# Interleaving side stages with a selective scan: another place on TensorE, earlier loads, another pacing rule

## The chip, the cores and the metric

The kernel runs on one core of a Trainium2 chip. The metric is the device time in microseconds (us) from the first to the last work of one execution. The kernel before took 11,412.55 us, the median of three runs (11,408.17 to 11,425.88). A core has five instruction streams that matter here: TensorE (PE in the profile; its weight loads are PEld), VectorE (DVE), ScalarE (ACT), GpSimd (POOL) and SyncE (SP), which issues every DMA of this kernel. Each works through its own queue in order.

## The reference, cut to what matters

Four images of 64 x 64 positions and 96 channels pass through four layers. Layer 0 and layer 1 are selective-scan blocks; layers 2 and 3 are attention without softmax, and a small feed-forward network with 8-bit rounding. Layer 1 takes a 2D Fourier transform first and its inverse after. In both blocks the core of the work is this recurrence, run in four directions over all positions, with 16 states for each channel:

```python
def step(hst, inputs):
    ul, dl, bl, cl = inputs
    dA = jnp.exp(dl[..., None] * A)
    hst = hst * dA + (dl * ul)[..., None] * bl[:, :, None, :]
    y = jnp.einsum('bkdn,bkn->bkd', hst, cl)
    return (hst, y)
```

Around it stand an input projection, a 3 x 3 convolution per channel, SiLU, small projections that give delta, B and C, and afterwards a layer norm, a gate (SiLU of a second projection) and an output projection.

## The kernel before, in words

**The scans.** The recurrence is cut into phases: two for layer 0 (two images packed in the 128 partitions each) and four for layer 1 (one image each). A phase has four directions; each direction is cut into segments of positions, eight of 512 in layer 0, and five of 512, 512, 384, 384 and 320 in layer 1. A segment has 12 steps: four groups of four states (q) times three chunks of 128 channels (c). So there are 384 steps in each of the first two phases and 240 in each of the other four, 1728 in all. A step runs four scans on VectorE (line 676), one per state.

For each scan ScalarE makes the decay, an exponential (`exp`, line 648; `front_x` for states 0 and 1, `front_y` for states 2 and 3, the latter in PSUM). The input term of states 0 and 1 is made position-major on ScalarE (`make_bx`, line 612) and turned by TensorE (`transposed`, line 644): these are the b transposes. For states 2 and 3 GpSimd multiplies it (`front_b`, line 666). The outputs are multiplied by C on GpSimd (`multiply`, line 713) or VectorE (`multiply_kept`, line 694), and TensorE adds them up in PSUM by transposing matmuls (`accumulate`, line 723). B and C come as broadcasts by DMA (line 590), two buffers each.

PSUM has eight banks: three for the accumulators, three (`ab0` to `ab2`) that the b transposes and the decays of states 2 and 3 share in turn, one for preparing the next segment (`pp`), and one (`ms`) for everything else. So transposes for state 0 of the next step wait until scan 1 of this step is done with its bank, and those for state 1 until scan 2 is.

**The side stages.** While a phase is scanned, stages of other images are woven in: for example the normalisation and projection of the second pair (`begin0`), its gate (`gate0`), the flip to the other direction (`flip`), the norm and output projection of a finished phase (`end0`, `end1`), the Fourier transform (`fourier`), its inverse, and the two transformer layers (`tokens`). Each is a Python generator; what lies between two `yield`s is a piece. `Env` keeps the stages in a queue, and `Env.step` issues one piece. A piece can ask for a place: `yield LATE` means only the last slot of a step, `yield BURST` means the place for a long ScalarE instruction (`burst`, after which a step's second slot is held back). A copy out of PSUM is deferred: it is issued at the next piece (`E.flush`).

Each of the four engines' orders is written out by hand (the loop over `steps`, line 809). A step has three slots, where `slot` issues one piece of the next segment's preparation (`prepare`) and, when the counter `due` has reached 1, one side piece. `due` grows in each slot by a third of the phase's rate, up to 3. The rates (`RATES`) are 1.75, 2.5, and 3.0 for the rest. On TensorE a step's order was: accumulations, transposes for state 0 of the next step, first slot, transposes for state 1, second slot, last slot. A stage that a phase needs is forced to its end before (`E.require`); what remains after the last scan is issued by `E.finish`.

Before and after the scans the first projection and the last stages run alone, several workers at once (`wide=4`): the head and the tail.

**Loads of side stages.** A stage loads its inputs through SP. `visits` loads rows of x two blocks ahead, but starts anew for each part and chunk: two loads, three empty pieces, then the matmuls. `flip` loads a part, waits two pieces, and has GpSimd turn it in eight LATE pieces; its input and output share two buffers (tag `h0`). `fourier` and `inverse` load two pieces ahead of the first use. `in_weights` loads a chunk's weights where the chunk begins.

Of the kernel before, what the change touches and what calls it, by code (L numbers as in the profile page):

```python
# [23 lines left out]
SM = 512  # L24
LATE, BURST = "late", "burst"

RATES = [1.75, 2.5, 3.0, 3.0, 3.0, 3.0]
EXP_LN = "natural_log_exp_and_others"


# [92 lines left out]
                active.remove(task)  # L123


class Block:


# [54 lines left out]
                    stop=(ki == cfg.KI - 1),  # L183
                )

    def visits(self, E, sp, wi, xf, blocks, half, nm, w, done):


        def load(r, n):
            x = sp.tile([CH, 2, 512], F32, name=f"xi{half}_{nm}_{r}", tag=f"xin{w}", bufs=3)  # L190
            self.nc.sync.dma_start(out=x[:, :, : n * 64], in_=xf[:, :, r * 64 : (r + n) * 64])
            return x
# [12 lines left out]

    def in_weights(self, sp, g, c, w):
        cfg = self.cfg
        wi = sp.tile([CH, cfg.KI, 2, cfg.PI], F32, name=f"{cfg.pre}_wi_{g}_{c}", tag=f"wi{w}", bufs=2)
        self.nc.sync.dma_start(out=wi, in_=self.w["inw"][:, :, :, c, :])
        return wi  # L210

    def project(self, E, g, io):

        nc, cfg = self.nc, self.cfg
        NR, xf, W = cfg.NR, io["xf"], min(E.wide, C)
        io["u"] = u = [self.dram_tile(f"u{j}", (P, C, cfg.L), g) for j in range(2)]
        PR = max(b - a for a, b in cfg.parts)

        def chunk(sp, c, w):
# [4 lines left out]
            wi = self.in_weights(sp, g, c, w)  # L226
            for p0, p1 in cfg.parts:
                nm, pr = f"{cfg.pre}_{g}_{c}_{p0}", p1 - p0
                pad = sp.tile([P, PR + 2, 66], F32, name=f"pad_{nm}", tag=f"pad{w}")
                nc.gpsimd.memset(pad[:, : pr + 2, 0:1], 0.0)  # L230
                nc.gpsimd.memset(pad[:, : pr + 2, 65:66], 0.0)
                if p0 == 0:
                    nc.gpsimd.memset(pad[:, 0, :], 0.0)
                if p1 == NR:
                    nc.gpsimd.memset(pad[:, pr + 1, :], 0.0)

                def to_pad(r, n, pi):
                    nc.scalar.copy(
                        pad[:, r - p0 + 1 : r - p0 + 1 + n, 1:65],
                        pi[:, : n * 64].rearrange("p (r w) -> p r w", w=64),  # L240
                    )

                lo, hi = max(p0 - 1, 0), min(p1 + 1, NR)
                blocks = [(r, min(8, hi - r)) for r in range(lo, hi, 8)]
                if blocks[-1][1] < 4 and len(blocks) > 1:
                    cut = hi - lo
                    k = len(blocks)
                    sizes = [cut // k + (i < cut % k) for i in range(k)]
                    blocks = [(lo + sum(sizes[:i]), s) for i, s in enumerate(sizes)]
                yield from self.visits(E, sp, wi, xf, blocks, 0, nm, w, to_pad)  # L250
                uh = sp.tile([P, PR * 64], F32, name=f"uh_{nm}", tag=f"h{w}", bufs=2)

                def to_u(r, n, pc):
                    nc.scalar.activation(
                        uh[:, (r - p0) * 64 : (r - p0 + n) * 64], pc[:, : n * 64], AF.Identity,
                        bias=self.conv_b[:, c : c + 1],
                    )

                for t in range(9 if vector else 0):
                    dy, dx = divmod(t, 3)  # L260
                    o = uh[:, : pr * 64].rearrange("p (r w) -> p r w", w=64)
                    v = pad[:, dy : dy + pr, dx : dx + 64]
# [24 lines left out]
                yield BURST  # L287
                nc.scalar.activation(uh[:, : pr * 64], uh[:, : pr * 64], AF.Silu)
                if W == 1:
                    nc.scalar.preload_act_table_set(EXP_LN)  # L290
                nc.sync.dma_start(out=u[cfg.nat][:, c, p0 * 64 : p1 * 64], in_=uh[:, : pr * 64])
                yield
                if W == 1:
                    yield from self.flip_part(sp, g, c, p0, p1, uh, u[1 - cfg.nat])

        with E.pool(f"{cfg.pre}pj{g}") as sp:
            yield from together([chunk(sp, c, c % W) for c in range(C)], W)
            if W > 1:
                nc.scalar.preload_act_table_set(EXP_LN)

    def flip_part(self, sp, g, c, p0, p1, uh, out):

# [13 lines left out]
    def flip(self, E, g, io):  # L316

        cfg = self.cfg
        PR = max(b - a for a, b in cfg.parts)
        with E.pool(f"{cfg.pre}fl{g}") as sp:  # L320
            for c in range(C):
                for p0, p1 in cfg.parts:
                    uh = sp.tile([P, PR * 64], F32, name=f"fl_{cfg.pre}_{g}_{c}_{p0}", tag="h0", bufs=2)
                    n = (p1 - p0) * 64
                    self.nc.sync.dma_start(out=uh[:, :n], in_=io["u"][cfg.nat][:, c, p0 * 64 : p1 * 64])
                    yield
                    yield
                    yield from self.flip_part(sp, g, c, p0, p1, uh, io["u"][1 - cfg.nat])
        yield

    def gate(self, E, g, io):
# [2 lines left out]
        io["gz"] = gz = self.dram_tile("gz", (P, C, cfg.L), g)  # L334
        PR = max(b - a for a, b in cfg.parts)
        with E.pool(f"{cfg.pre}gt{g}") as sp:
            for c in range(C):
                wi = self.in_weights(sp, g, c, 0)
                for p0, p1 in cfg.parts:
                    nm, pr = f"{cfg.pre}_{g}_{c}_{p0}", p1 - p0  # L340
                    zh = sp.tile([P, PR * 64], F32, name=f"zh_{nm}", tag="h0", bufs=2)
# [4 lines left out]
                    blocks = [(r, n) for r, n in cfg.rows if p0 <= r < p1]  # L346
                    yield from self.visits(E, sp, wi, io["xf"], blocks, 1, nm, 0, to_z)
# [142 lines left out]
def scans(tc, ctx, phases, ident):  # L490
# [274 lines left out]
    with tc.manual_schedule(engines=IN_ORDER):  # L765
# [20 lines left out]
        def slot(kind, hold=False):  # L786
# [22 lines left out]
        for i, st in enumerate(steps):  # L809
# [188 lines left out]
def fourier(E, cst, x, b, dram, out):  # L998
# [7 lines left out]
    with E.pool(f"ff{b}") as sp:  # L1006
# [9 lines left out]
            return t  # L1016

        nxt = load(0)
        yield
        yield  # L1020
# [33 lines left out]
def inverse(E, cst, att, x, b, x1):  # L1054
# [6 lines left out]
    with E.pool(f"fi{b}") as sp:  # L1061
# [45 lines left out]
            yield from together([channels(w * G, a, w) for w, a in enumerate(loads)], W)  # L1107
        else:
            nxt = load(0)
            yield  # L1110
            yield
# [459 lines left out]
```

## Time and profile before

| what | value |
|---|---|
| runs | 11,408.17, 11,412.55 and 11,425.88 us |
| profiled execution, its own time | 11,418.96 us |
| its span, from the first to the last instruction | 11,417.2 us |
| mean granted TensorE clock | 0.894 |
| first scan starts, last scan ends | 213.9 us, 11,011.7 us |
| phases 1 to 6 (scan to scan) | 2476.0, 2482.2, 1517.7, 1445.7, 1441.2, 1435 us |
| scans, mean of one | 1124 to 1263 ns for 512 positions |
| `multiply` on GpSimd, mean of one | 2642 ns |
| `front_b` on GpSimd, mean of one | 1169 ns |
| flip piece on GpSimd (L308), median | 627 ns |

In the profile, a group is named by line, engine and what it writes and reads (`h_l<-ab_l`). A wait stands as "who <- who released it: us in total, times, longest". In the timeline a row is start, duration, engine, line, operation, names, shapes, and in brackets the idle time before it and what ended that. The chain of waits goes back from the last instruction to whatever released it, or to the instruction before it on its engine; its share says what the end of the kernel stood on.

### The profile page before, as it was taken

Reading aid. Unit: us, or ns where it says so; the run is one execution under the profiler, and the core shown is the slowest. Engines: PE = TensorE matmul, PEld = TensorE weight load, DVE = VectorE, ACT = ScalarE, POOL = GpSimd, SP = SyncE. Lnnn points to the kernel's source line nnn. Section 1 sums busy time; section 2 is a strip of 40 time slices with the busy share of each in tenths; the row PEclk is TensorE's granted clock in tenths of the full one; section 3 lists DMA queues with packets and bytes.
Section 4 is the critical chain, followed back from the end, with each engine's and each line's share of the span. In section 5 each row is a group of like instructions: output and inputs, shape, how many; then the busy total and the mean of one; then the engine's idle time right before and its main releaser. Section 6 shows DMA issues by size and latency. Waiting matters only on the chain. (4 is left out here: it accounts for less than half of the span.)

```text
span 11417.2 us, 163659 instructions
## 1 busy us (share of the span) xinstructions
PE 9108.9 (80%) x54944; PEld 6661.7 (58%) x54944; DVE 9922.7 (87%) x10695; ACT 9367.1 (82%) x19648; POOL 9402.0 (82%) x7464
## 2 busy tenths in 40 slices
PE   5668878788888878888888888887778877887775
PEld 2555555555666656556665565665556556665554
DVE  6889999889998998999878687988999899889964
ACT  4779999999988998998768777878888798878853
POOL 2899999988988998998779688887888788888850
PEclk9889999988998999998889899998899988998887
DMA  4555554556665455555543443542244422542242
GB/s 142 131 140 127 130 132 123 144 154 167 160 166 127 130 143 130 134 140 165 156 125 122 123 133 121 172 129 88 97 121 148 110 94 97 151 130 97 87 124 40
DMA packets 1208403, 1468.94 MB, mean 129 GB/s; under 512 B 482760, under 2 KB 1020560, under 8 KB 1149064
## 3 DMA queue, kind: packets, MB, share of 16 engines
q1 hardware_dynamic: 1207559, 1458.48, 47.0%
q8 instruction: 434, 7.11, 0.3%
q14 instruction: 410, 3.35, 0.1%
HBM read 1221.74 MB, written 236.50 MB: 128 GB/s over the span
## 5 line engine op out<-in xcount | busy, mean ns | idle before, releaser
L713 POOL TENSOR_TENSOR h_l<-h_l,bc_l 128x1536 f32<-128x1536 f32 (+2 forms) x1728 | 4565.0, 2642 | 203.2 <-DVE h_l L676 87.4
L666 POOL TENSOR_TENSOR h_l<-du_l,bc_l 128x512 f32<-128x512 f32 (+2 forms) x3456 | 3964.8, 1169 | 859.1 <-PE acc_l L723 806.4
L612 ACT ACTIVATE bx_l<-dut_l,bt_l 128x192 f32<-128x192 f32 (+2 forms) x6272 | 2750.8, 499 | 0.2
L723 PE MATMUL acc_l<-ident,h_l 128*128 128x128 f32 (+1 forms) x15840 | 2365.1, 302 | 257.0 <-POOL h_l L713 255.8
L723 PEld LDWEIGHTS acc_l<-ident,h_l 128*128 128x128 f32 (+1 forms) x15840 | 2065.1, 157 | 843.2 <-POOL h_l L713 389.5
L648 ACT ACTIVATE ax_l<-delta_l,l_alog 128x512 f32<-128x512 f32 (+2 forms) x3456 | 2140.4, 667 | 0.0
L676 DVE TENSOR_TENSOR_SCAN h_l<-b_l,state_l,h_l 128x512 f32<-128x512 f32 (+2 forms) x1266 | 1398.7, 1124 | 195.5 <-ACT b_l L648 181.7
L644 PE MATMUL b_l<-ident,bx_l 128*128 128x128 f32 (+1 forms) x6830 | 1233.9, 298 | 350.8 <-DVE h_l L676 339.4
L644 PEld LDWEIGHTS b_l<-ident,bx_l 128*128 128x128 f32 (+1 forms) x6830 | 834.8, 150 | 840.3 <-DVE h_l L676 628.3
L648 ACT ACTIVATE b_l<-delta_l,l_alog 128x512 f32<-128x512 f32 (+2 forms) x1952 | 1222.8, 626 | 102.5 <-DVE k_l L694 32.0
L644 PE MATMUL ab_l<-ident,bx_l 128*128 128x128 f32 x5320 | 916.0, 301 | 278.8 <-DVE h_l L676 265.9
L723 PE MATMUL acc_l<-ident,k_l 128*128 128x128 f32 x5121 | 838.5, 294 | 340.4 <-DVE k_l L694 323.8
L676 DVE TENSOR_TENSOR_SCAN b_l<-ax_l,state_l,b_l 128x512 f32<-128x512 f32 (+2 forms) x844 | 956.0, 1133 | 136.7 <-PE b_l L644 136.2
L648 ACT ACTIVATE ab_l<-delta_l,l_alog 128x512 f32<-128x512 f32 x1328 | 914.8, 689 | 146.3 <-DVE hk_l L694 62.5
L676 DVE TENSOR_TENSOR_SCAN h_l<-ab_l,state_l,h_l 128x512 f32<-128x512 f32 x744 | 925.3, 1263 | 113.3 <-ACT ab_l L648 64.5
L644 PEld LDWEIGHTS ab_l<-ident,bx_l 128*128 128x128 f32 x5320 | 655.4, 153 | 579.4 <-DVE h_l L676 474.2
L676 DVE TENSOR_TENSOR_SCAN h_l<-ax_l,state_l,b_l 128x512 f32<-128x512 f32 (+2 forms) x844 | 953.7, 1130 | 38.6 <-PE b_l L644 37.4
L694 DVE TENSOR_TENSOR k_l<-b_l,bc_l 128x512 f32<-128x512 f32 (+2 forms) x1462 | 896.5, 613 | 62.6 <-DMA bc_l<-l_xd_l 9.1
L723 PEld LDWEIGHTS acc_l<-ident,k_l 128*128 128x128 f32 x5121 | 632.2, 150 | 437.5 <-DVE k_l L694 356.2
L723 PE MATMUL acc_l<-ident,hk_l 128*128 128x128 f32 x3984 | 647.4, 300 | 249.6 <-DVE hk_l L694 237.7
L276 PE MATMUL pc_l<-pad_l,l_dg 128*128 128x512 f32 (+2 forms) x1656 | 771.1, 560 | 40.2 <-ACT state_l L701 22.0
L694 DVE TENSOR_TENSOR hk_l<-ab_l,bc_l 128x512 f32<-128x512 f32 x996 | 688.9, 692 | 54.5 <-issue 11.1
(252 smaller groups left out, 14802.7 us busy)
## 6 DMA issues: line engine op xcount, KB each, us to landing
bc_l<-l_xd_l SPq DMA_DIRECT2D x640, 512.0 KB
bc_l<-l_xd_l SPq DMA_DIRECT2D x512, 256.0 KB
bc_l<-l_xd_l SPq DMA_DIRECT2D x128, 1024.0 KB
bc_l<-l_xd_l SPq DMA_DIRECT2D x128, 768.0 KB
us_l<-l_u SPq DMA_DIRECT2D x96, 768.0 KB
l_y<-y_l SPq DMA_DIRECT2D x288, 256.0 KB
yt_l<-l_y SPq DMA_DIRECT2D x264, 192.0 KB
yt_l<-l_y SPq DMA_DIRECT2D x128, 384.0 KB
```

Of the source, the lines that this page charges most:

```text
L276: nc.tensor.matmul(pc[:, : n * 64].rearrange("p (r w) -> p r w", w=64), diag[:, t, :], pad[:, r - p0 + dy : r - p0 + dy + n, dx : dx + 64] ...
L612: nc.scalar.activation(t[:n, b, :, ch], z.dut[:n, b, :, ch], AF.Copy, scale=z.bt[:n, b, m : m + 1])
L644: nc.tensor.transpose(pb[:, t : t + n], st.z.bx[st.q, j][:n, b, st.c], ident[:n, :n])
L648: nc.scalar.activation(out, z.delta[:, st.c, : z.S], AF.Exp, scale=z.blk.A[:, st.c, z.k, n : n + 1])
L666: nc.gpsimd.tensor_tensor(st.h[:, 1 + j, :S], st.z.du[:, st.c, :S], st.z.b[st.q][:, j, :S], ALU.mult)
L676: nc.vector.tensor_tensor_scan(h[:, ::step], a[:, ::step], b[:, ::step], 0.0 if z.first else z.state[st.c][:, n : n + 1], ALU.mult, ALU.add,)
L694: nc.vector.tensor_tensor(hk[:, : z.S], kept_at(st, j), z.c[st.q][:, j, : z.S], ALU.mult)
L713: nc.gpsimd.tensor_tensor(h, h, z.c[st.q][:, 1 : 1 + m, : z.S], ALU.mult)
L723: nc.tensor.matmul(z.acc[st.c][:m, b, :], hc[:, t : t + m], ident, start=(first and b == 0), stop=(last and b == 0), is_transpose=True,)
```

## The change

Three things change, and no arithmetic does.

1. In a step, the first slot now comes before the transposes for state 0, and the second before those for state 1.
2. Side stages load further ahead. The new class `Inputs` holds the loads of a whole projection or gate: two blocks of rows are always ahead, across parts and chunks, and eight empty pieces stand once at the start in place of three at each part. `flip` loads the next part while it turns this one, with a buffer tag of its own and eight empty pieces at the start. `fourier` and `inverse` have six empty pieces in place of two.
3. The rates are 0.15 lower, and a slot may issue a second side piece when `due` is at least 2.

```diff
-RATES = [1.75, 2.5, 3.0, 3.0, 3.0, 3.0]
+RATES = [1.6, 2.35, 2.85, 2.85, 2.85, 2.85]
...
+class Inputs:
+    def __init__(self, blk, sp, xf, chunks, half, nm, w):
+        self.blk, self.sp, self.xf, self.half, self.nm, self.w = blk, sp, xf, half, nm, w
+        self.todo = [
+            (c, r, n) for c in chunks for p0, p1 in blk.cfg.parts for r, n in blk.rows_of(p0, p1, half == 0)
+        ]
+        self.ahead, self.wi = [], {}
+        for _ in range(2):
+            self.load()
+
+    def load(self):
+        if not self.todo:
+            return
+        sp, cfg, nc = self.sp, self.blk.cfg, self.blk.nc
+        c, r, n = self.todo.pop(0)
+        if c not in self.wi:
+            t = sp.tile([CH, cfg.KI, 2, cfg.PI], F32, name=f"{cfg.pre}_wi_{self.nm}_{c}", tag=f"wi{self.w}", bufs=2)
+            nc.sync.dma_start(out=t, in_=self.blk.w["inw"][:, :, :, c, :])
+            self.wi[c] = t
...
+        nc.sync.dma_start(out=x[:, :, : n * 64], in_=self.xf[:, :, r * 64 : (r + n) * 64])
+        self.ahead.append((self.wi[c], x))
+
+    def take(self):
+        self.load()
+        return self.ahead.pop(0)
...
-        ahead = [load(*blk) for blk in blocks[:2]]
-        yield
-        yield
-        yield
-        for b, (r, n) in enumerate(blocks):
-            ahead += [load(*blk) for blk in blocks[b + 2 : b + 3]]
-            x = ahead.pop(0)
...
+        for r, n in blocks:
+            wi, x = inputs.take()
             pi = E.psum(f"pi{half}_{nm}_{r}")
             yield from self.in_proj(pi, wi, half, x, n * 64)
             E.defer(lambda r=r, n=n, pi=pi: done(r, n, pi))
...
-            yield from together([chunk(sp, c, c % W) for c in range(C)], W)
-            if W > 1:
-                nc.scalar.preload_act_table_set(EXP_LN)
+            if W == 1:
+                inputs = Inputs(self, sp, xf, range(C), 0, g, 0)
+                for _ in range(8):
+                    yield
+                for c in range(C):
+                    yield from chunk(sp, inputs, c, 0)
+                return
+            yield from together([chunk(sp, Inputs(self, sp, xf, [c], 0, g, c), c, c) for c in range(C)], W)
+            nc.scalar.preload_act_table_set(EXP_LN)
...
+        todo = [(c, p0, p1) for c in range(C) for p0, p1 in cfg.parts]
         with E.pool(f"{cfg.pre}fl{g}") as sp:
...
+            nxt = load(*todo[0])
+            for _ in range(8):
+                yield
+            for n, (c, p0, p1) in enumerate(todo):
+                uh, nxt = nxt, load(*todo[n + 1]) if n + 1 < len(todo) else None
+                yield from self.flip_part(sp, g, c, p0, p1, uh, io["u"][1 - cfg.nat])
...
             due = min(due + st.z.ph.rate / 3, 3.0)
-            if due >= 1.0:
+            for _ in range(min(int(due), 1 + (due >= 2.0))):
                 due -= E.step(kind)
...
+            slot(None)
+            if nxt:
                 transposed(nxt, 0)
-            slot(None)
             more.take(skip=long)
             scan(st, 2)
+            slot(None, hold=long)
             if nxt:
                 transposed(nxt, 1)
-            slot(None, hold=long)
             if older and older.q == NQ - 1:
                 close_chunk(older)
             scan(st, 3)
...
-            yield
-            yield
+            for _ in range(6):
+                yield
             for c0 in range(0, CH, G):
```

The gate stage takes its rows from an `Inputs` too, the cutting of rows into blocks moves into `rows_of`, and the last part of the diff stands in `fourier` and, alike, in `inverse`.

More of the change, by code (lines that the diff above doesn't have):

```diff
@@ L123, in together @@
                 active.remove(task)
+class Inputs:
[16 more added lines that the diff above has]
+            self.wi[c] = t
+        x = sp.tile(
+            [CH, 2, 512], F32, name=f"xi{self.half}_{self.nm}_{c}_{len(self.todo)}", tag=f"xin{self.w}", bufs=3
+        )
+        nc.sync.dma_start(out=x[:, :, : n * 64], in_=self.xf[:, :, r * 64 : (r + n) * 64])
[3 more added lines that the diff above has]
+        return self.ahead.pop(0)
 class Block:
@@ L184, in in_proj, with rows_of, visits @@
                 )
[L186 to L192, printed above, removed]
-        ahead = [load(*blk) for blk in blocks[:2]]
-        yield
-        yield
-        yield
-        for b, (r, n) in enumerate(blocks):
-            ahead += [load(*blk) for blk in blocks[b + 2 : b + 3]]
-            x = ahead.pop(0)
+    def rows_of(self, p0, p1, halo):
+        cfg = self.cfg
+        if not halo:
+            return [(r, n) for r, n in cfg.rows if p0 <= r < p1]
+        lo, hi = max(p0 - 1, 0), min(p1 + 1, cfg.NR)
+        blocks = [(r, min(8, hi - r)) for r in range(lo, hi, 8)]
+        if blocks[-1][1] < 4 and len(blocks) > 1:
+            cut = hi - lo
+            k = len(blocks)
+            sizes = [cut // k + (i < cut % k) for i in range(k)]
+            blocks = [(lo + sum(sizes[:i]), s) for i, s in enumerate(sizes)]
+        return blocks
+    def visits(self, E, inputs, blocks, half, nm, done):
+        for r, n in blocks:
+            wi, x = inputs.take()
             pi = E.psum(f"pi{half}_{nm}_{r}")
@@ L204, in visits @@
             yield
[L206 to L210, printed above, removed]
     def project(self, E, g, io):
@@ L219, in project, with chunk @@
         PR = max(b - a for a, b in cfg.parts)
-        def chunk(sp, c, w):
+        def chunk(sp, inputs, c, w):
             vector = W > 1 and c > 0
@@ L225, in chunk @@
                 nc.sync.dma_start(out=diag, in_=self.diag[:, c])
-            wi = self.in_weights(sp, g, c, w)
             for p0, p1 in cfg.parts:
@@ L241, in to_pad @@
                     )
[L243 to L250, printed above, removed]
+                yield from self.visits(E, inputs, self.rows_of(p0, p1, True), 0, nm, to_pad)
                 uh = sp.tile([P, PR * 64], F32, name=f"uh_{nm}", tag=f"h{w}", bufs=2)
@@ L319, in flip, with load @@
         PR = max(b - a for a, b in cfg.parts)
+        todo = [(c, p0, p1) for c in range(C) for p0, p1 in cfg.parts]
         with E.pool(f"{cfg.pre}fl{g}") as sp:
[L321 to L325, printed above, removed]
-                    yield
-                    yield
-                    yield from self.flip_part(sp, g, c, p0, p1, uh, io["u"][1 - cfg.nat])
+            def load(c, p0, p1):
+                uh = sp.tile([P, PR * 64], F32, name=f"fl_{cfg.pre}_{g}_{c}_{p0}", tag="fl", bufs=2)
+                n = (p1 - p0) * 64
+                self.nc.sync.dma_start(out=uh[:, :n], in_=io["u"][cfg.nat][:, c, p0 * 64 : p1 * 64])
+                return uh
+            nxt = load(*todo[0])
[4 more added lines that the diff above has]
+                yield from self.flip_part(sp, g, c, p0, p1, uh, io["u"][1 - cfg.nat])
         yield
@@ L336, in gate @@
         with E.pool(f"{cfg.pre}gt{g}") as sp:
+            inputs = Inputs(self, sp, io["xf"], range(C), 1, g, 0)
+            for _ in range(8):
+                yield
             for c in range(C):
-                wi = self.in_weights(sp, g, c, 0)
                 for p0, p1 in cfg.parts:
@@ L344, in to_z @@
                         nc.scalar.copy(zh[:, (r - p0) * 64 : (r - p0 + n) * 64], pz[:, : n * 64])
-                    blocks = [(r, n) for r, n in cfg.rows if p0 <= r < p1]
-                    yield from self.visits(E, sp, wi, io["xf"], blocks, 1, nm, 0, to_z)
+                    yield from self.visits(E, inputs, self.rows_of(p0, p1, False), 1, nm, to_z)
                     yield BURST
@@ L1018, in fourier @@
         nxt = load(0)
-        yield
-        yield
+        for _ in range(6):
+            yield
         for c0 in range(0, CH, G):
@@ L1109, in inverse @@
             nxt = load(0)
-            yield
-            yield
+            for _ in range(6):
+                yield
             for c0 in range(0, CH, G):
```

## The prediction

> **What bounds the kernel now.** I read the busy shares first.
>
> ```profile
> PE 9108.9 (80%) x54944; PEld 6661.7 (58%) x54944; DVE 9922.7 (87%) x10695; ACT 9367.1 (82%) x19648; POOL 9402.0 (82%) x7464
> ```
>
> No engine is full, so I took the busy times by stage (columns: window, length, then busy us and count for PE, PEld, DVE, ACT, POOL; granted clock; DMA share; GB/s). The first scan starts at 214 us and the last ends at 11,012; phases 1, 3 and 6 are shown, and two short stretches.
>
> ```profile
> 214.00:2690.00 2476.00, 1906.52 (x10838) 1351.59 (x10839) 2240.62 (x2137) 2192.93 (x4696) 2309.82 (x1711) 0.90 0.54 135
> 5172.00:6690.00 1518.00, 1303.42 (x7833) 965.33 (x7832) 1238.45 (x1410) 1150.23 (x2285) 1189.59 (x1013) 0.88 0.47 136
> 9577.00:11012.00 1435.00, 1143.25 (x7123) 842.17 (x7121) 1316.67 (x1535) 1200.17 (x2496) 1209.40 (x1014) 0.89 0.37 111
> 2000.00:2070.00 70.00, 60.11 (x365) 41.97 (x363) 69.38 (x68) 65.48 (x130) 68.65 (x42) 1.00 0.46 117
> 6526.00:6549.00 23.00, 23.00 (x195) 19.33 (x194) 12.35 (x11) 10.50 (x21) 11.14 (x9) 0.63 0.51 73
> ```
>
> In layer 0 a segment without trouble takes 69.8 us and VectorE and GpSimd fill it (69.38 and 68.65 of 70). In phase 3 TensorE is the fullest (1303 of 1518), and in heavy stretches it alone works (23.00 of 23). So the limit changes from stretch to stretch, and what can be won is waiting. Next, the waits (us, times, longest):
>
> ```profile
> POOL h_l L666 <- PE acc_l L723: 806.4, 442, 14.4
> PEld b_l L644 <- DVE h_l L676: 628.3, 951, 4.2
> PEld ab_l L644 <- DVE h_l L676: 474.2, 686, 8.7
> ACT dut_l L581 <- PE pp_l L578: 302.1, 279, 12.3
> DVE b_l L676 <- PE b_l L644: 161.6, 97, 11.4
> DVE ab_l L676 <- PE ab_l L644: 125.0, 78, 11.1
> PE pi_l L178 <- DMA xi_l<-xf: 46.0, 12, 8.9
> ```
>
> The b transposes (L644) wait for a scan, with the slot's side work queued behind them; ScalarE waits for side work (L581, and smaller rows like it: 767 waits for TensorE, 1280 us in all); VectorE sometimes waits for the transposes. A stretch of the timeline (start, us) shows the first of these loops:
>
> ```profile
> 5856.00 0.66 PE L644 MATMUL ab_l<-ident,bx_l 128*128 128x128 f32 x4
> 5857.57 1.80 PE L1026 MATMUL pfz<-fw,xw 64*64 64x33 f32 x24
> 5859.42 0.49 ACT L1032 COPY z<-pfz 128x396 f32<-128x396 f32 x1 [6.94 <-PE pfz L1026]
> 5860.60 1.28 DVE L676 TENSOR_TENSOR_SCAN h_l<-ab_l,state_l,h_l 128x512 f32<-128x512 f32 x1 [2.63 <-ACT ab_l L648]
> ```
>
> Transposes, then side matmuls, then the copy that waits for them, then the exponential behind the copy, then a scan that waits. And a flip in phase 1 (of 6):
>
> ```profile
> 340.45 7.06 SPq L325 DMA_DIRECT2D fl_l<-l_u  x1
> 354.22 0.60 POOL L308 COPY ut_l<-fl_l 128x256 f32<-128x256 f32 x1 [5.66 <-DMA fl_l<-l_u]
> 355.75 0.69 DVE L694 TENSOR_TENSOR hk_l<-ab_l,bc_l 128x512 f32<-128x512 f32 x1 [6.33 <-DMA bc_l<-l_xd_l]
> ```
>
> GpSimd waits for a load issued too late, and the B/C broadcast queued behind its 7 us issue makes VectorE wait too.
>
> For shares I followed the chain of waits back from the end, restarting it where the profile loses it. Over the 10,798 us of scans: POOL about 2260 us, ACT 2620, PE 2560, DVE 2030, DMA 460, the rest issue.
>
> **Part 1: loads further ahead.** No bytes are added. The loads that the change moves stood on the chain with 220 us: fl 59 (with its issue), x rows (xi, and the xf stores before them) 113, xw 19, at and the att stores before it 28. What they truly cost is less, since another path is next: I compared each hit step (with its two neighbours) with the median of the steps around it, capped by the chain's share: fl 34, xi and xf 58, xw 19, at 27, together 138 us, 63% of the chain's figure. The lead grows from two or three pieces to six or eight (at 2.85 pieces a step and 6 us a step, 13 to 17 us; a load that stalled took 5 to 14), and across parts to two visits. On SP the moved loads pass B/C broadcasts at 0.57 us each (L191), which slack covers; the flips' 7 us issue still stands ahead of some broadcast, and if that cover is missing, up to 6.33 us at five places stay. I take fl 20, xi 45, xw 15, at 20: **100 us** (bounds 50 and 138). The one new wait, a flip load for its own buffer, ends with the GpSimd copies that the store ahead of it on SP waits for anyway: 0. The head has one such wait, 2.3 us before a matmul at 140.0 us; I take 0.
>
> **Part 2: side work ahead of the transposes.** Only TensorE's order changes: the slots' copies, adds and DMAs keep their places on the other queues, the transposes are TensorE's alone. I gave each TensorE instruction its slot by program order: the first slot holds side or preparation matmuls in 1169 of 1728 steps, the second in 910.
> Gain: side work no longer queues behind 0.66 us of transposes and their wait for a scan. Where the chain leaves TensorE from a slot of the first two kinds with the slot's own transposes before it, those transposes and that wait sum to 225 us (235 places, 0.96 us each). At the 63% of Part 1: 135 us.
> Cost: the transposes now come behind the side work, and behind whatever that waits for (TensorE idles 204 us inside these slots, for a load or for the bank's last copy). Queued behind a waiting side matmul are now the transposes; who waits for those is the next step's scans 0 and 1. I compared each slot's length beyond the transposes with the slack until the scan that reads them plus TensorE's idle time before them: at 622 places it doesn't fit, 558 us in all. Of these, 285 us lie in phases 3 and 4, where TensorE carries most of the chain (674 and 484 us): there its work per step is the same in either order, and a late scan makes it wait for nothing; I count 0. Of the other 273 I count VectorE's share of the chain from 10,100 us to the last scan, 26%: 72 us.
> Net: **63 us** won; bounds 225 won and, all shortfalls real and no gain, 558 lost. I stay near the small figure because both ends are first-order sums and the slack row is wide (median 1.1 to 1.9 us before scan 0, 1.5 to 2.3 before scan 1, against side work of 1.0 us).
>
> **Part 3: rates and the second piece.** I counted pieces from the code. Before, 4024 are due and 31 are left after the last scan; begin0 and each gate0 lose 10, flip0 4, each begin1 gains 2, each end1 4: 4010. The slot rule followed through the 1728 steps with these counts ends the side work at step 1718, with 194 double slots, 180 of them LATE ones. So the leftover goes:
>
> ```profile
> 11012.00:11045.00 33.00, 15.90 (x80) 9.67 (x80) 6.53 (x10) 10.32 (x17) 4.58 (x5) 0.60 0.81 199
> 11020.70 0.36 SPq L369 DMA_DIRECT2D yt_l<-l_y  x1
> ```
>
> The tail's first matmul starts at 11,045.1, its first load at 11,020.7, and such loads take 8 to 10 us on the chain: **15 us** (5 to 25). Spreading pieces brings nothing by itself: layer-0 steps with one, two and three pieces took 6.5, 6.3 and 6.6 us on average. A second piece that uses the one side bank must wait for the copy of the first, with the next step's accumulation queued behind it and GpSimd behind that: near rows are py after yb's copy, 30.2 us in 35 waits, 0.86 us each. The Trainium skill (Perfetto Trace Analysis, Optimization Strategy) speaks against the second piece here: bubbles that repeat can mean that PSUM lacks room for the next tile. By that rule every double slot would lose a bubble, 194 times 0.86, 167 us; by the rows most doubles are GpSimd flips or norms without a bank, and each leaves a lighter slot elsewhere. I take 0 (20 won to 80 lost).
>
> **The clock.** The Trainium skill (TensorE: Matmul & The Clock Gate, Part 1) says that activity releases the throttle, full speed when busy for some 3.4 us. By that, closing TensorE's gaps would lift 0.894 towards 1: 0.106 of the 2560 us on the chain, 271 us. The rows disagree: 0.63 where TensorE was busy for all 23 us, 1.00 where it was busy for 60 of 70. I take 0 from the clock.
>
> **Sum.** 100 + 63 + 15 = 178 us off the profiled execution's 11,418.96 us (span 11,417.2): 11,241. The median shown, 11,412.55, is 6.4 lower, so **11,235 us**, 1.6% faster.
>
> **The rivals.**
> (B) Side round trips pay in full and late transposes cost nothing: 138 + 225 + 20 = 383, about 11,030. For it: ACT waits 1280 us for PE. Against: the shortfalls.
> (C) The reorder does nothing to the end (ScalarE's saved wait turns into one for VectorE's scan 0, already L701's 309 us): 100 + 15, about 11,300.
> (D) Slower: transposes late for scans 0 and 1. It decides when over 250/558, 45%, of the shortfall reaches VectorE (135 + 100 + 15 won against it); at 65%, 363 lost, about 11,525. For it: VectorE is the fullest engine, and already waits 287 us for L644. Against: where TensorE is late, it is mostly the bound itself.
>
> **How the numbers follow.** Likeliest 0.48 (11,150 to 11,310), B 0.15, C 0.25, D 0.12. A measurement of this kernel tells apart about 0.2%, 23 us. Faster by more: 0.84; within: 0.06 (the ends of C and D); slower: 0.10. The range 11,060 to 11,400 leaves out half of B and most of D.
>
> **What would show it.** Right: the waits of L308 and L178 for DMA nearly gone; L581 and its like well under 1280 us; PEld L644 for DVE well under 1100; the py matmul within 20 us of the last scan; DVE for PE L644 below some 400 us. Wrong: DVE for L644 doubled (D); ACT's waits for PE unchanged (C); POOL for acc above 806, from the double slots.

## The result, and the profile after

| | runs | median, us | ratio to before, 95% interval |
|---|---|---|---|
| before | 6 | 11,417.74 | 1 |
| changed | 6 (11,300.14 to 11,343.17) | 11,317.6 | 0.9911 (0.9901 to 0.9922) |

The change takes 0.89%, some 102 us (0.0089 x 11,415 us, about what the kernel before took in every series: medians of 11,413 to 11,418), off the kernel. The forecast was 178 us and 11,235 us. The profiled execution took 11,308.41 us, its span is 11,306.6 us and the granted clock 0.900. The end lies closest to rival C (11,300), in which the reorder on TensorE does nothing, and just beyond the stretch called likeliest (11,150 to 11,310).

The changed file is longer: 676 (scan) is now 710, 644 (b transposes) 678, 648 (exponential) 682, 666 (`front_b`) 700, 723 (accumulate) 757, 694 (`multiply_kept`) 728, 701 (`keep_state`) 735, 581 (the dut copy) 615, 308 (the flip copy) 335 and 178 (input projection) 210. First the busy shares, then the stages (phases 1, 3, 5 and 6; columns as in the prediction):

```profile
PE 9021.5 (80%) x54944; PEld 6600.5 (58%) x54944; DVE 9899.2 (88%) x10695; ACT 9384.7 (83%) x19648; POOL 9405.2 (83%) x7464
```

```profile
217.00:2668.00 2451.00, 1878.85 (x10846) 1330.00 (x10846) 2235.99 (x2136) 2200.67 (x4702) 2310.04 (x1711) 0.91 0.55 137
5112.00:6582.00 1470.00, 1289.69 (x7829) 952.53 (x7828) 1233.57 (x1410) 1152.68 (x2285) 1189.87 (x1013) 0.89 0.49 141
8007.00:9476.00 1469.00, 1161.77 (x7218) 857.55 (x7219) 1322.87 (x1552) 1233.10 (x2565) 1213.62 (x1016) 0.88 0.37 111
9476.00:10912.00 1436.00, 1133.90 (x7114) 832.02 (x7113) 1312.84 (x1531) 1200.14 (x2489) 1209.19 (x1013) 0.89 0.37 112
```

The work is the same to within a per cent, so the gain is waiting. It is uneven: phases 1 to 4 went from 2476, 2482, 1518 and 1446 us to 2451, 2444, 1470 and 1426; phase 5 got longer, from 1441 to 1469, and phase 6 stayed at 1435. The waits (us, times, longest):

```profile
POOL h_l L700 <- PE acc_l L757: 718.1, 419, 7.9
PEld b_l L678 <- DVE h_l L710: 476.8, 752, 4.4
PEld ab_l L678 <- DVE h_l L710: 452.4, 678, 6.1
ACT dut_l L615 <- PE pp_l L612: 290.8, 274, 6.5
DVE b_l L710 <- PE b_l L678: 257.4, 200, 8.5
ACT state_l L735 <- DVE hk_l L728: 207.4, 186, 11.6
ACT state_l L735 <- DVE k_l L728: 194.7, 226, 4.5
DVE ab_l L710 <- PE ab_l L678: 130.5, 84, 6.9
DVE h_l L710 <- ACT b_l L682: 124.5, 124, 3.5
```

Three of these have rows of before that the prediction did not show:

```profile
DVE h_l L676 <- ACT b_l L648: 215.8, 240, 3.5
ACT state_l L701 <- DVE hk_l L694: 179.6, 167, 10.7
ACT state_l L701 <- DVE k_l L694: 129.8, 145, 6.0
```

All five signs that the prediction named came out on its side. The L308 and L178 rows for loads of `fl_l` and `xi_l<-xf` are gone from the list. ScalarE's waits for TensorE, all rows added, fell from 1280 to 961 us. The transposes' waits for scans fell from 628 + 474 to 477 + 452. VectorE waits 257 + 131 = 388 us for the transposes, just under 400. GpSimd's wait for the accumulators fell from 806 to 718. The tail's first matmul starts at 10,927.2 us, 15.6 after the last scan ends. And yet 76 of the 178 us are missing, so these signs did not ask the right question. The scan waits less for ScalarE (216 to 125 us) and more for TensorE (162 + 125 to 257 + 131), and ScalarE waits more for VectorE (309 to 402). One stretch of the changed kernel's timeline shows how:

```profile
6153.82 1.86 PE L210 MATMUL pi_l<-xi,l_wi 96*128 96x448 f32 x2
...
6155.47 1.84 PE L678 MATMUL b_l<-ident,bx_l 128*128 128x128 f32 x6
6155.47 0.23 PEld L678 LDWEIGHTS b_l<-ident,bx_l 128*128 128x128 f32 x1 [0.52 <-issue]
...
6155.71 0.53 ACT L266 COPY pad_l<-pi_l 128x448 f32<-128x448 f32 x1 [1.20 <-PE pi_l L210]
...
6156.44 0.89 DVE L710 TENSOR_TENSOR_SCAN b_l<-ax_l,state_l,b_l 128x320 f32<-128x320 f32 x1 [3.30 <-PE b_l L678]
```

The 1.86 us of side matmuls now go first. ScalarE's copy waits only 1.20 us for them (6.94 in the stretch of before, which is of another stage), but the scan waits 3.30 us for the transposes behind them.

### The profile page after: what moved, and what is told of

Its sections match the earlier page's. It is cut to its first block, busy times and chain, and to the rows that moved or that the text cites. A ratio compares the mean times of both kernels' runs of the same rounds, so it can differ in the third digit from the quotient of the medians.

```text
span 11306.6 us, 163986 instructions
## 1 busy us (share of the span) xinstructions
PE 9021.5 (80%) x54944; PEld 6600.5 (58%) x54944; DVE 9899.2 (88%) x10695; ACT 9384.7 (83%) x19648; POOL 9405.2 (83%) x7464
## 5 line engine op out<-in xcount | busy, mean ns | idle before, releaser
L757 PE MATMUL acc_l<-ident,h_l 128*128 128x128 f32 (+1 forms) x15840 | 2326.3, 299 | 135.9 <-POOL h_l L747 135.6
L678 PE MATMUL b_l<-ident,bx_l 128*128 128x128 f32 (+1 forms) x6817 | 1200.5, 295 | 227.1 <-DVE h_l L710 220.2
L757 PE MATMUL acc_l<-ident,k_l 128*128 128x128 f32 (+1 forms) x5117 | 836.9, 294 | 334.3 <-DVE k_l L728 320.1
L757 PEld LDWEIGHTS acc_l<-ident,k_l 128*128 128x128 f32 (+1 forms) x5117 | 627.3, 150 | 437.2 <-DVE k_l L728 368.7
L757 PEld LDWEIGHTS acc_l<-ident,hk_l 128*128 128x128 f32 x3976 | 494.1, 152 | 409.7 <-DVE hk_l L728 337.3
```

Source lines behind the costliest of these rows:

```text
L678: nc.tensor.transpose(pb[:, t : t + n], st.z.bx[st.q, j][:n, b, st.c], ident[:n, :n])
L757: nc.tensor.matmul(z.acc[st.c][:m, b, :], hc[:, t : t + m], ident, start=(first and b == 0), stop=(last and b == 0), is_transpose=True,)
```

## The experiments

All kernels were timed against the kernel before. A phase is the stretch from its first scan to the next phase's first scan in the profiled run.

| kernel | median, us | ratio, 95% interval |
|---|---|---|
| order only | 11,428.29 | 1.0013 (1.0005 to 1.0021) |
| first slot ahead only | 11,424.55 | 1.0009 (1.0000 to 1.0018) |
| second slot ahead only | 11,422.72 | 1.0007 (0.9999 to 1.0016) |
| loads only | 11,311.21 | 0.9906 (0.9893 to 0.9920) |
| flip loads only | 11,374.72 | 0.9969 (0.9957 to 0.9981) |
| x rows only | 11,387.89 | 0.9976 (0.9968 to 0.9983) |
| pacing only | 11,451.47 | 1.0030 (1.0020 to 1.0040) |
| loads and pacing, no order | 11,306.14 | 0.9905 (0.9890 to 0.9919) |
| the same, no pair in the norm | 11,294.85 | 0.9891 (0.9876 to 0.9905) |
| loads, second piece, old rates | 11,433.09 | 1.0016 (1.0009 to 1.0023) |
| loads, pacing in phases 1 to 3 | 11,241.32 | 0.9853 (0.9838 to 0.9869) |
| the same, order in phases 3 to 6 | 11,222.02 | 0.9832 (0.9816 to 0.9848) |

My theory was that the loads pay as forecast and the order pays nothing, since ScalarE's waits turn into VectorE's (C). The rivals were that the order pays and the pacing eats it, and that the loads pay less than counted.

### The order alone, and its two halves

The order alone, on the kernel before:

```diff
-                transposed(nxt, 0)
             slot(None)
+            if nxt:
+                transposed(nxt, 0)
             more.take(skip=long)
             scan(st, 2)
+            slot(None, hold=long)
             if nxt:
                 transposed(nxt, 1)
-            slot(None, hold=long)
```

> The kernel before with only the order on TensorE changed: slot one ahead of the transposes for state 0, slot two ahead of those for state 1; loads, rates and the slot rule as before. As predicted (order worth 63 us): about 11,355 us, 0.55% under the kernel before, ScalarE's waits for TensorE inside the scans down by some 300 us. Rival N (the saved waits of ScalarE turn into waits of VectorE for late transposes): within 20 us of the kernel before, DVE for PE up by as much as DVE for ACT goes down. Rival D (transposes late): slower by 50 us or more.

Measured: 0.13% slower, some 15 us, which is rival N's end. Its waits:

```profile
DVE b_l L676 <- PE b_l L644: 356.6, 219, 10.8
...
ACT state_l L701 <- DVE k_l L694: 206.8, 210, 7.7
ACT state_l L701 <- DVE hk_l L694: 204.0, 199, 10.5
DVE ab_l L676 <- PE ab_l L644: 189.1, 116, 9.1
...
DVE h_l L676 <- ACT b_l L648: 107.0, 117, 3.3
```

VectorE waits 357 + 189 = 546 us for the transposes, 1.9 times the 287 of before: nearly the sign set for D. With all rows between the first and the last scan added, ScalarE's waits for TensorE fell by 142 us (939 to 797) and VectorE's for ScalarE by 222 (434 to 212), but VectorE's for TensorE rose by 277 (405 to 682), ScalarE's for VectorE by 139 (541 to 680) and TensorE's for ScalarE by 93 (354 to 447). VectorE, the fullest engine, lost 55 us more on these two than it gained; its other waits fell by 36 us, so it stood idle 19 us longer. The phases changed by +8.5, +21.5, -5, -7, +1 and -6 us: it costs in layer 0, where VectorE and GpSimd fill the time. There VectorE's waits for TensorE rose by 117 us and those for ScalarE fell by only 58; in layer 1 it was 166 against 163.

One half each, the first on the first slot and the second on the second slot:

```diff
-                transposed(nxt, 0)
             slot(None)
+            if nxt:
+                transposed(nxt, 0)
```

> The kernel before with only the first slot moved ahead of its transposes (for state 0, read by the next step's first scan, whose slack has a median of 1.1 to 1.9 us). Theory N (saved ScalarE waits return as VectorE waits for transposes): VectorE waits for TensorE up by some 140 of the 277 us that both slots together cost, time within 20 us of the kernel before. If slack decides alone, this half is the dearer one: 10 to 30 us slower.

```diff
             scan(st, 2)
+            slot(None, hold=long)
             if nxt:
                 transposed(nxt, 1)
-            slot(None, hold=long)
```

> The kernel before with only the second slot moved ahead of its transposes (for state 1, read by the second scan; median slack 1.5 to 2.3 us). Theory N: the rest of the 277 us of VectorE waits, time within 20 us. If slack decides alone, this half is the cheaper one and gains 5 to 25 us.

Measured: 0.09% and 0.07% slower, some 10 and 8 us, the second not to be told from no change. Between first and last scan VectorE's waits for TensorE are 631 and 620 us (before 405), for ScalarE 269 and 241 (before 434). This leaves out one wait of some 50 us before the very first scan, on which more below. Each half makes the same trade, so no good half was spoilt by a bad one. Each alone adds over 200 of the 277 us, not some 140, and the second did not gain the 5 to 25 us that its slack had suggested.

### The loads alone, and their parts

The changed kernel with the old order, rates and slot rule:

```diff
-RATES = [1.6, 2.35, 2.85, 2.85, 2.85, 2.85]
+RATES = [1.75, 2.5, 3.0, 3.0, 3.0, 3.0]
...
-            for _ in range(min(int(due), 1 + (due >= 2.0))):
+            if due >= 1.0:
                 due -= E.step(kind)
```

> The kernel before with only the loads of side stages further ahead. As predicted: 100 us faster, about 11,317. Rival N needs nearly all of the measured gain here: 85 to 115 us. If the order gave 63 us after all and the loads were overrated: 25 to 50 us.

Measured: 0.94% faster, 107 us, as much as the whole change brings. Waits for DMA between first and last scan fell on TensorE from 136 to 41 us and on GpSimd from 37 to 5. VectorE's go from 102 to 50, but only because its wait before the very first scan, at the end of the head, is put down to a DMA in one profile and to ScalarE in the other (before, then the loads alone):

```profile
213.94 1.23 DVE L676 TENSOR_TENSOR_SCAN ab_l<-ax_l,ab_l 128x512 f32<-128x512 f32 x1 [48.62 <-DMA bc_l<-l_xd_l]
```

```profile
215.60 1.23 DVE L710 TENSOR_TENSOR_SCAN ab_l<-ax_l,ab_l 128x512 f32<-128x512 f32 x1 [51.19 <-ACT ax_l L682]
```

Without that wait VectorE's are 53 and 50 us. So 130 us fewer of waits went with 107 us less time, a ratio of 0.82. (The 0.6 in the next expectation took that wait for a gain.)

The flip's loading alone (the diff's part in `flip`, on the kernel before):

```diff
+            nxt = load(*todo[0])
+            for _ in range(8):
+                yield
+            for n, (c, p0, p1) in enumerate(todo):
+                uh, nxt = nxt, load(*todo[n + 1]) if n + 1 < len(todo) else None
```

> The old kernel with the flip's changed loading alone (first load eight pieces ahead, the next one a part ahead, a tag of its own). The prediction put it at 20 us of gain (11,395). If GpSimd's wait for these loads (37 us inside the scans before, 5 after) lies on the path at the 0.6 that all loads together showed: 20 us less. Rival: the flip's buffer of its own lets side work run on sooner and denser, and gains nothing, as the second piece did: within 5 us of before.

The x rows alone (the kernel with the loads alone, but with the flip's loading of before and, as shown, the two Fourier loads of before):

```diff
-        for _ in range(6):
-            yield
+        yield
+        yield
         for c0 in range(0, CH, G):
```

> The old kernel with the input rows and input weights of project and gate loaded ahead across parts and chunks, alone; flip and the two Fourier loads stay as they were. The prediction put these rows at 45 us of gain and the Fourier loads at 15, of 100 with the flip and what goes with it. Additive: about 11,350 to 11,370. If TensorE's waits for DMA are the larger part (136 to 41 us inside the scans with all loads): up to 80 us less, and the flip next to nothing.

Measured: 35 us for the flip (0.0031 x 11,415; 20 were expected) and 27 for the x rows (45 or more were expected). The flip's waits on GpSimd, 33.0 us before and all in phase 1, are gone in its kernel, and in its profile phase 1 is 45 us shorter. In the x-row kernel they are still there, beside those for the Fourier loads and what is left of the x rows' (46.0 us before):

```profile
PE piv L1110 <- DMA at<-att: 43.8, 6, 26.4
...
POOL ut_l L335 <- DMA fl_l<-l_u: 34.7, 5, 7.8
PE pfz L1054 <- DMA xw<-x: 26.8, 3, 10.9
...
PE pi_l L210 <- DMA xi<-xf: 22.0, 8, 5.9
```

So 33 us of GpSimd waits went with 35 us. TensorE's waits for DMA fell by 56 us with the x rows (136 to 80), but what that was worth can't be read here: the profiled execution took 11,414 us, 26 above its kernel's median and only 5 below the profiled one of before. The remaining 45 of 107 would be the two Fourier loads with what the parts do together; they were not run alone. In the changed kernel the next flip load is issued while the last part is still being turned:

```profile
324.51 0.64 POOL L335 COPY ut_l<-fl_l 128x256 f32<-128x256 f32 x1
325.60 7.04 SPq L353 DMA_DIRECT2D fl_l<-l_u  x1
331.21 0.64 POOL L335 COPY ut_l<-fl_l 128x256 f32<-128x256 f32 x1
338.04 1.20 POOL L335 COPY ut_l<-fl_l 128x256 f32<-128x256 f32 x2
```

The 7 us of issue on SP stay, but no copy shows a wait.

### Pacing

The rates and the second piece on the kernel before:

```diff
-RATES = [1.75, 2.5, 3.0, 3.0, 3.0, 3.0]
+RATES = [1.6, 2.35, 2.85, 2.85, 2.85, 2.85]
...
-            if due >= 1.0:
+            for _ in range(min(int(due), 1 + (due >= 2.0))):
                 due -= E.step(kind)
```

> The kernel before with only the lower rates and the second piece in a slot. As predicted: 15 us faster from the leftover pieces after the last scan (tail shorter by 10 to 15), nothing in the scans. If double slots make the one side bank a bubble: slower by up to 80 us in phases 5 and 6, where the norms of the transformer layers fall.

The changed kernel with the order put back (loads and pacing):

```diff
+                transposed(nxt, 0)
             slot(None)
-            if nxt:
-                transposed(nxt, 0)
...
-            slot(None, hold=long)
             if nxt:
                 transposed(nxt, 1)
+            slot(None, hold=long)
```

> The changed kernel with the old order on TensorE, so loads and pacing together. As predicted: 63 us slower than the changed kernel, about 11,380. Rival N: equal to the changed kernel within 20 us. Rival D: faster than the changed kernel by 30 us or more.

Measured: alone 0.30% slower, some 34 us. By phase that is -25, +15, -27, +3, +58 and +24 us, and -13 in the tail: the tail as predicted, and in phases 5 and 6 a loss of the size and in the place that the expectation gave to a bubble at the side bank. On top of the loads the pacing brings nothing (11,306 against 11,311). That nothing is a sum: by phase, loads and pacing against loads alone, -13, -42, -19, +7, +64 and +12 us, and -12 in the tail, where the leftover pieces had been. The next two kernels ask for the loss in phase 5. In its norm, the second piece puts VectorE's piece and the ScalarE square that reads it into one slot (the columns are start, us, engine, line; loads and pacing):

```profile
8823.15 0.96 DVE L1225 SCALAR_TENSOR_TENSOR xn<-lnm_2a,tok 128x768 f32<-128x768 f32 x1
8824.03 1.28 DVE L710 TENSOR_TENSOR_SCAN ab_l<-ax_l,state_l,ab_l 128x512 f32<-128x512 f32 x1
8824.15 0.84 ACT L1240 ACTIVATE lnq_2a<-xn 128x768 f32<-128x768 f32 x1 [2.05 <-DVE xn L1225]
```

ScalarE stands 2.05 us at the head of a step. Such waits sum to 53 us here and to 0 with one piece a slot. Without that pair:

```diff
-            for _ in range(min(int(due), 1 + (due >= 2.0))):
+            for again in range(min(int(due), 1 + (due >= 2.0))):
+                if again and kind is LATE and E.wants is None:
+                    break
                 due -= E.step(kind)
```

> Loads and pacing, old order on TensorE, but no second piece after a LATE piece that is followed by an ordinary one; so a VectorE piece of a norm and the ScalarE piece that reads it no longer share a slot. Stages end at the same steps by count; only 51 of the 194 double slots go. Theory P (the pair makes ScalarE stand at the head of the next step until VectorE is through): ScalarE's idle time before the squares back from 53 us to about 0, the 60 steps around norms from 8.0 to 7.3 us, 30 to 45 us faster than loads and pacing together, about 11,265. Rival Q (phases 5 and 6 are longer because heavier pieces fall on other steps): within 15 us of loads and pacing together.

And with the second piece, but the old rates (from loads and pacing):

```diff
-RATES = [1.6, 2.35, 2.85, 2.85, 2.85, 2.85]
+RATES = [1.75, 2.5, 3.0, 3.0, 3.0, 3.0]
```

> Loads further ahead and the second piece, with the old higher rates and the old order on TensorE. If the lower rates are what helps phases 1 to 3 (74 us there between loads alone and loads with pacing): those phases go back to the loads' times, and with the norms' pairs still there the kernel is 40 to 80 us slower than loads alone, about 11,360. If the second piece is what helps them: phases 1 to 3 stay within 20 us of loads with pacing, about 11,305.

Measured: without the pair the waits before the squares are gone, and the time falls by 11 us, with overlapping intervals, not by 30 to 45; phase 5 is still 1484 us, so the pair is not the main cause (rival Q). With the old rates the kernel is 122 us slower than with the loads alone (40 to 80 were expected): 8 us less in phases 1 to 3, 150 more in phases 4 to 6, 17 less in the tail. So the second piece by itself does not win the 74 us of phases 1 to 3; the lower rates are needed for it. Whether they would do it with one piece a slot was not run. Against loads and pacing, the old rates cost 41, 54 and 18 us in phases 3, 4 and 6 and nothing in phase 5. Phase 5 with loads alone, and with loads and pacing:

```profile
8048.00:9473.00 1425.00, 1153.75 (x7226) 857.50 (x7227) 1324.12 (x1550) 1222.69 (x2577) 1204.89 (x1008) 0.89 0.37 114
```

```profile
7983.00:9472.00 1489.00, 1172.13 (x7219) 859.12 (x7219) 1328.88 (x1553) 1231.17 (x2566) 1214.14 (x1017) 0.88 0.36 109
```

VectorE's work differs by 5 us, the length by 64, and its waits for TensorE make 46 of that. GpSimd waits longer for the accumulators. And TensorE has waits that were not there, before small matmuls of the transformer layers (`ph`), until VectorE has copied out what the side bank held, which for `x` is also their input (the same two windows):

```profile
POOL h_l L700 <- PE acc_l L757: 96.0, 71, 5.5
```

```profile
POOL h_l L700 <- PE acc_l L757: 139.7, 85, 7.1
...
PE ph L1304 <- DVE h L1315: 13.0, 13, 1.6
PE ph L1304 <- DVE x L1298: 11.5, 12, 1.4
```

Over the whole scan these `ph` waits come to 54 us, all in phases 4 to 6 (0.3 with the loads alone), and to 26 without the pair. That they make the loss is not shown: the last kernel below has 71 us of them in the same phases and is the fastest. Which pieces collide was not settled. Of the 64 us, 30 lie in 24 steps that hold little but the inverse transform under the old pacing; under the new one the first pieces of a transformer layer come into them too.

The last two kernels use this. Pacing only where it paid, from the kernel with the loads alone:

```diff
-RATES = [1.75, 2.5, 3.0, 3.0, 3.0, 3.0]
+RATES = [1.6, 2.35, 2.85, 3.0, 3.0, 3.0]
...
-            if due >= 1.0:
+            for _ in range(min(int(due), 1 + (due >= 2.0 and st.z.ph.rate < 3.0))):
```

> The loads of the change with the old transpose order, and the new pacing (lower rate, second piece) in the first three phases only; phases 4 to 6 keep one piece a slot at rate 3. If phases don't influence one another, the pacing gains what it gained there over the loads alone (12.6 + 41.8 + 19.5 = 74 us) and the 82 us that it cost in phases 4 to 6 go: about 11,311 - 74 = 11,237 us. Rival: the second piece only shifts side work, so that what the first phases save comes back in the later ones, because pieces that the first phases leave over or take early change what is left for the later: then it stays within 25 us of 11,311 whatever the phases. The six phases are compared one by one: phases 1 to 3 should be near 2440, 2436, 1457 and phases 4 to 6 near 1426, 1425, 1427.

And, in addition, the new order in layer 1 alone:

```diff
+                if z.cfg is CFG0:
                     transposed(nxt, 0)
             slot(None)
+            if nxt and z.cfg is CFG1:
+                transposed(nxt, 0)
             more.take(skip=long)
             scan(st, 2)
-            if nxt:
+            if nxt and z.cfg is CFG0:
                 transposed(nxt, 1)
             slot(None, hold=long)
+            if nxt and z.cfg is CFG1:
+                transposed(nxt, 1)
```

> The kernel with pacing in phases 1 to 3, with side work ahead of the transposes only in phases 3 to 6 (layer 1), where VectorE is less full. With the change's order put on the old kernel these four phases went by -5, -7, +1 and -6 us, and on loads with pacing by +13, -7, -20 and -4. If the order pays where VectorE has room: 10 to 30 us less than the kernel without it. If the saved ScalarE waits turn into VectorE waits there too: within 10 us of it.

Measured: 11,241 us (expected 11,237), then 11,222. The first is 61 us better than the loads alone by the ratios (0.9906 - 0.9853), with phases of 2439, 2441, 1469, 1440, 1428 and 1423 us: what the pacing cost later stays away, except for some 14 us in phase 4. (These phases are of a profiled execution of 11,263 us, 22 above the median.) Phase 5 is back:

```profile
8003.00:9432.00 1429.00, 1147.83 (x7228) 849.88 (x7229) 1322.50 (x1549) 1225.65 (x2584) 1204.15 (x1008) 0.89 0.37 114
```

The order in layer 1 brings 19 us more, inside the 10 to 30 expected; the two intervals overlap a little, so the gain is likely and not certain. Phases 3 to 6 went by +2, -16, -9 and -8 us, but phase 2, whose order is the same in both, by -9 too. In the earlier two pairs of kernels the order took 17 us off phases 3 to 6 each time, one profile each. The waits without and with it:

```profile
DVE h_l L710 <- ACT b_l L682: 203.1, 216, 3.8
DVE b_l L710 <- PE b_l L678: 119.1, 101, 3.6
...
DVE ab_l L710 <- PE ab_l L678: 77.9, 52, 6.3
```

```profile
DVE b_l L710 <- PE b_l L678: 206.8, 172, 3.6
DVE h_l L710 <- ACT b_l L682: 143.8, 139, 3.8
DVE ab_l L710 <- PE ab_l L678: 130.6, 85, 6.9
```

The same trade is there: with all rows of phases 3 to 6 added, VectorE's waits for ScalarE fall from 289 to 131 us and those for TensorE rise from 224 to 375. It is about even here, as it was in layer 1 of the kernel before (166 against 163); the loss there was in layer 0. With 11,222 us, 1.68% below before, this is the fastest kernel of the study; the change as made reached 0.89%.

## Why the prediction was right in sign and wrong in size

**Part 1, loads: right in the sum, with luck.** 100 us forecast, 107 measured, of 220 on the chain. The waits for these loads were on the path, as the part said. Its division was not right: the flip gave 35 for 20, the x rows 27 for 45, and the rest 45 for 35 (xw 15 and at 20; the expectation for the x rows names only the 15). Three errors of 10 to 18 us nearly cancel. Waits may count more on an engine that is full, as GpSimd is in layer 0 (68.65 of 70 us), so that one factor for all engines would be wrong; the runs don't show that.

**Part 2, order: the step that failed.** It put the gain at 135 us and the cost at 72, net 63. Alone it cost 15 us, and on top of loads and pacing it was worth nothing: 7 to 11 us slower, within the intervals. The gain was there as waits: ScalarE waited 142 us less for TensorE. Two of its figures don't follow from what stands beside them: 63% of 225 is 142, not 135, and 26% is the share of the scans alone (L676) on the chain of that last stretch, where all of VectorE's lines have 35%. With both put right it would have been 142 less 95, still 47 won. The mis-sized term is the cost: "Of the other 273 I count VectorE's share of the chain from 10,100 us to the last scan, 26%: 72 us", after leaving out 285 us where TensorE is fullest. VectorE's waits for TensorE rose by 277 us, nearly four times 72; 62 of it in phase 3 and 41 in phase 4, where I had counted 0. They ate the 222 us by which its waits for ScalarE fell: in phases 3 and 4 one for one (63 and 42 us), in layer 0 twice over (117 against 58), and there the time was lost. On top of loads and pacing it was -184 against +238, the first wait left out. That is rival C's mechanism, with a little of D in layer 0.

**Part 3, pacing: the sum was right by accident.** 15 us from the tail were forecast, 12 measured there. For the rest I took 0, and with the loads it is 0. But it is 74 us won in phases 1 to 3 and 82 lost in phases 4 to 6, and without the loads it costs. The rule of the Trainium skill (Perfetto Trace Analysis, Optimization Strategy), from which I reckoned 167 us of bubbles for want of PSUM before I took 0, was partly right: waits for the side bank came up, 54 us before `ph`, all in phases 4 to 6. GpSimd's waits for TensorE hide it in the total, 750 us with the loads alone and 719 with the pacing added, but they fell by 71 in phases 1 to 3 and rose by 40 in phases 4 to 6. How much of the 82 us these waits make stays open. The pair in the norm, ScalarE behind VectorE's piece, had no bank in it, and without it the time fell by 11 us, within the intervals. Why pacing gains 42 us in phase 2 with the loads and loses 15 without them was not tried.

**The clock.** 0 was right as far as one profile each can say: TensorE's busy time fell from 9109 to 9021 us in the changed kernel and only to 9101 with the loads alone, at the same end time. The granted clock was 0.894 before, 0.900 in the changed kernel and 0.904 in the fastest one. The two rows that I held against the rule can't tell cause from effect: a matmul of a b transpose (L644) took 354 ns on average where the clock was 0.63, and 280 where it was 1.00, so a low clock by itself makes TensorE look full.

**Sum.** 107 (loads) less some 9 (order) and plus 1 to 5 (pacing) is about 102. Of the 76 us missing from the forecast of 178, the order accounts for 63 + 9; the rest are errors of a few us that nearly cancel.

## What to carry to other kernels

Moving work on one in-order queue to let one consumer run earlier makes another consumer run later: before counting the gain, add up both consumers' waits at the engine that sets the pace, stage by stage, because here 222 us won met 277 lost, while in the whole change each sign that I had set for success was met. Earlier loads were the safe part here: 130 us fewer of waits went with 107 us. Before summing waits by releaser, look at the longest: one of 50 us changed its releaser from profile to profile. Split a pacing rule by stage before judging it: a zero in the total was -74 and +82.

## What was not expected

- The parts do not add up: alone they come to 0.51% (0.94 - 0.13 - 0.30), together to 0.89%. The pacing costs 0.30% on the kernel before and nothing once the loads are early.
- Allowing two pieces in a slot at unchanged rates cost 1.1% (0.9906 to 1.0016), more than the earlier loads brought (0.94%).
- The flip's SP issue of 7 us stayed, and so did VectorE's waits for B/C broadcasts in phase 1 (18 us before, 20 with the flip change alone, the first wait left out); the flip's gain did not need them to go.
